# Four graph layers on one core: another load path for the neighbour counts, a pinned place for small loads, and another order for the last bank

## The chip, the cores and the metric

The kernel runs on one core of a Trainium2 chip. The metric is device time in microseconds for the whole program, the median of five runs. Beside it stands one profiled execution, whose trace gives every time quoted below: times in the trace count from the start of its span.

## The reference

Four layers work on x (3,327 nodes by 512 features) and one 0/1 adjacency matrix. Each layer's result is added to its input, and each row is then normed (mean taken off, divided by its deviation).

```
Layer 0 (attention, 8 heads of 64): Wh = x W; e[i,j] = leaky(f1[i] + f2[j]); where adj[i,j] > 0
        softmax over j, weights times Wh
Layer 1 (mean of neighbours): of each row keep the first 64 neighbours; nb = their mean of x;
        x <- norm(x + leaky(x Wl' + bl) + (leaky(nb Wn' + bn) where the row has a neighbour, else 0))
Layer 2 (as layer 0, other weights, then elu)
Layer 3 (as layer 2, 4 heads of 128)
```

Layer 1 needs for each row the number of its neighbours, as min(count, 64), its reciprocal, and whether it is above 0. These counts are what the change calls the neighbours' counts.

## The kernel before, in words

Rows are worked on in 26 tiles of 128 (NT = 26; the last tile holds 127 rows). A layer's attention runs over two halves of 13 tiles (HALF) of rows i and four slots s of 128 output features. One such (half, s) is a unit: it goes over all 26 tiles of neighbours j, makes a weight tile on VectorE (L403) and its sigmoid on ScalarE (L406), and multiplies on TensorE into the four banks `po` (L426, numerators) and the banks `pd` (L378, denominators). At a unit's end `po` is copied to `ob`, transposed by TensorE in groups of four tiles (`QUADS`: tiles 0 to 3, 4 to 7, 8 to 11 and 12) through `transposed` (L451), and either stored to `hd` in device memory (L464) or handed to `final` (L992). The denominators become `rec`, the reciprocals that the numerators are multiplied with.

TensorE's instructions keep the order in which they are written. All other engines and queues are ordered by a planner when the program is built, by priority in the order of writing and by its own idea of when inputs are ready; `tc.keep_in_program_order(ins)` pins an instruction behind the one written last on the same engine, without a wait for its end. An engine or a queue then works strictly in that order. SP issues DMAs from `nc.sync`, POOL those from `nc.gpsimd`.

**Start of layer 1** (`sage`, L676). The counts of all rows lie in device memory in row NT of `ctd`, as bf16. They are loaded by POOL into `cb` (L741) with rows on partitions, so each element goes to a place of its own, and turned into `cnt` on VectorE (L751 to L753); the first is pinned and written at tile 8. The loop from L745 takes tiles in twos. `finish` loads `h` and `xr` of the next two tiles (L126: the first group from POOL, later `h` from SP), multiplies with `rec` (L181), adds (L195), takes statistics (L152, L153) and norms (L154 to L161). `step1` transposes a tile on TensorE (L714) into the PSUM tile `pt`, of which there are two; `step2` of the tile before it makes two products (L722, L725) and stores `zd` and `xid`. In TensorE's order: step 1 of tile t, step 2 of tile t - 1.

**Late denominators.** For the last unit of layers 0 and 2 (`end` in `unit`) the denominators go out as `dd` (L505) and come back as `pes` by 16 small DMAs on SP (`place`, L508 to L515), written where the loop of the next stage (`sage`, or `third` at L907) has come to tile 4. At tile 8 `finish_sums` (L521 to L534, pinned) makes `rec` of the second half from them.

**Start of layer 3** (`third`, L878). The same pattern with `load_group` (L897), ten `h` buffers, `project1` (L251) and `project2` (L264), which stores `v` (L281) by SP; each normed tile is stored to x3 by SP (L133).

**The tail** (L992 to L1030). For layer 3's second half the finished output stays on chip in `g`; only slot s = 3 is left at the end. `take` divides a group out of PSUM into `h` (L999), takes exp (L1002), adds twice (L1004, L1005) and takes the row statistics (L1008, L1009). The groups 0 and 1 are transposed first, then `sums` and `reciprocals` make `rec` (L559 to L569), then the takes follow. After them come two blocks, tiles 0 to 7 and 8 to 12: one square root (L1019), two small steps for `rs` (L1020, L1021), and for each tile, from the last to the first, the scaling (L1026 on ScalarE for every fourth, else L1028 on VectorE) and the store (L133, L131; even tiles by SP, odd ones by POOL).

Of the kernel before, what the change touches and what calls it, by code (L numbers as in the profile page):

```python
# [18 lines left out]
P = 128  # L19
# [13 lines left out]
def kernel(  # L33
# [190 lines left out]
    class Layer:  # L224
# [137 lines left out]
        def unit(self, pools, half, s, background, aside, final=None, ending=None):  # L362
# [127 lines left out]
            if not by_pe:  # L490
# [17 lines left out]
                def place(pool=sp, tag="red", eng=nc.gpsimd):  # L508
                    pes = pool.tile([P, HALF, 2, 2, NS], F32, name="pes", tag=tag, bufs=1)
                    held.append(pes)  # L510
                    for kk in range(4):
                        q0, nq = (0, NA) if kk < 2 else (NA, HALF - NA)
                        src = dd[32 * kk:32 * kk + 32, :4 * nq].rearrange("i (q m) x -> m i q x", m=4)
                        for m in range(4):
                            eng.dma_start(out=pes[32 * m:32 * m + 32, q0:q0 + nq, kk % 2]  # L515
                                          .rearrange("p q o s -> p q (o s)"), in_=src[m])
# [54 lines left out]
            if not final:  # L571
# [3 lines left out]
            return [lambda: take.append(transposed(*QUADS[0])), lambda: take.append(transposed(*QUADS[1])),  # L575
                    sums, reciprocals] + [lambda q=q: take[q]() for q in range(2)] + \
                [lambda q=q: transposed(*q)() for q in QUADS[2:]]
# [98 lines left out]
    def sage(first, first_pool, xin, prev, nxt, wsrc, dst):  # L676
# [3 lines left out]
        with tc.tile_pool(name="sg_z", bufs=1, reuse_waits="tile") as zp, \  # L680
# [21 lines left out]
            with tc.tile_pool(name="sa_w", bufs=1, reuse_waits="tile") as wp, \  # L702
# [37 lines left out]
                cb = zp.tile([P, NT], BF, name="cb")  # L740
                nc.gpsimd.dma_start(out=cb, in_=ctd[NT:NT + 1, :].rearrange("o (t p) -> p (o t)", p=P))  # L741
# [3 lines left out]
                for t0 in range(0, NT, 2):  # L745
# [3 lines left out]
                    if t0 == 8:  # L749
                        tc.keep_in_program_order(  # L750
                            nc.vector.tensor_scalar(cnt[:, 0, :], cb, NEIGHBOURS, 1.0, op0=ALU.min, op1=ALU.max))  # L751
                        nc.vector.reciprocal(cnt[:, 1, :], cnt[:, 0, :])
                        nc.vector.tensor_scalar(cnt[:, 2, :], cb, 0.0, None, op0=ALU.is_gt)  # L753
# [124 lines left out]
    def third(first):  # L878
        with tc.tile_pool(name="col3", bufs=1) as cp, tc.tile_pool(name="at_r3", bufs=2, reuse_waits="tile") as rp:
# [51 lines left out]
            with tc.tile_pool(name="f3", bufs=2) as fp, tc.tile_pool(name="f4", bufs=1) as gp:  # L931
# [60 lines left out]
                def final(s, q0, n, pt):  # L992
# [4 lines left out]
                    def take():  # L997
                        h = fp.tile([P, 4, P], F32, name="h", bufs=2)
                        nc.vector.tensor_tensor(h[:, :n], pt[:, :n], rec[:, HALF + q0:HALF + q0 + n, s:s + 1]  # L999
                                                .to_broadcast([P, n, P]), op=ALU.mult)  # L1000
                        e = fp.tile([P, 4, P], F32, name="e")
                        nc.scalar.activation(e[:, :n], h[:, :n], AF.Exp)  # L1002
                        y = g[:, qs, s * P:(s + 1) * P]
                        nc.vector.scalar_tensor_tensor(y, e[:, :n], 1.0, y, op0=ALU.min, op1=ALU.add)  # L1004
                        nc.vector.scalar_tensor_tensor(y, h[:, :n], 0.0, y, op0=ALU.max, op1=ALU.add)  # L1005
                        if s == NS - 1:
                            for q in range(q0, q0 + n):
# [176 lines left out]
```

## Time and profile before

| What | us |
|---|---|
| median of 5 runs (lowest, highest) | 3392.05 (3390.57, 3394.94) |
| the profiled execution's own time | 3392.05 |
| its span | 3390.3 |
| PE busy | 3249.6 (96%) |
| DVE busy | 2684.2 (79%) |
| ACT busy | 2356.8 (70%) |
| last attention product of layer 0, start of layer 1 | about 957 |
| last product of layer 1's first loop's tile 0 | about 969.9 |
| last products of layer 3's attention | about 3360 |

PE is TensorE, DVE VectorE, ACT ScalarE, POOL GpSimd; SPq and POOLq are the queues of SP and POOL. A line of a timeline gives the start, the duration, the engine, the line of the kernel, the operation, the tile written and the tile read, the number of instructions, and in brackets the idle time before it with what ended it ("issue" where the view names nothing). A line of the waits gives who waited for what: total, times, longest.

### The profile page before, as it was taken

How to read it: one execution, taken by the hardware profiler on the slowest of the kernel's cores; microseconds unless marked ns; L12 is line 12 of the kernel's file. 1: busy time of each engine (PE TensorE's matmuls, PEld its weight loads, DVE VectorE, ACT ScalarE, POOL GpSimd, SP SyncE). 2: the span in 40 equal slices, each digit the busy share in tenths (PEclk: the TensorE clock that was granted, in tenths of full speed). 3: DMA queues.
4: the chain of work that ended last, by engine and by line, in shares of the span. 5: the costliest groups of instructions: out<-in, count | busy, mean ns of one | idle time of the engine just before them, and what ended most of it. 6: DMA issues, size and time to landing. Idle time of an engine off the chain costs nothing.

```text
span 3390.3 us, 47140 instructions
## 1 busy us (share of the span) xinstructions
PE 3249.6 (96%) x18423; PEld 1626.5 (48%) x18475; DVE 2684.2 (79%) x2615; ACT 2356.8 (70%) x2142; POOL 241.7 (7%) x390
## 2 busy tenths in 40 slices
PE   8799999999979999999989999999998999999997
PEld 7544344444434445545544444444446754445453
DVE  5799999999967544444449999999998766668886
ACT  2398998999953333333329999999997755558985
POOL 3100000000010011111110000000002000010110
PEclk9999999999989999999999999999999999999998
DMA  9644111110143343333320111111117411122311
GB/s 372 216 126 126 49 49 39 57 46 28 44 122 120 116 122 88 90 83 87 84 77 19 48 50 48 50 50 42 38 32 238 155 41 42 41 51 78 96 42 49
DMA packets 288055, 284.29 MB, mean 84 GB/s; under 512 B 107533, under 2 KB 223575, under 8 KB 287832
## 3 DMA queue, kind: packets, MB, share of 16 engines
q1 hardware_dynamic: 254024, 170.61, 16.7%
q0 software_dynamic: 28288, 102.97, 9.7%
q10 hardware_dynamic: 5520, 7.69, 0.7%
q8 instruction: 146, 2.39, 0.3%
q14 instruction: 77, 0.63, 0.1%
HBM read 212.01 MB, written 69.17 MB: 83 GB/s over the span
## 4 chain that ended last, share of the span: by engine, by line
PE 84%; DVE 4%; DMA 4%; issue 4%; ACT 3%; POOL 0%; SPq 0%; ACTq 0%; POOLq 0%; DVEq 0%
PE po L426 50%; PE acc L845 12%; PE pd L378 7%; PE pw L269 5%; DVE t L403 3%; PE pz L722 3%; PE pi L725 3%; DMA raw<-in_adjT_dram 2%; ACT y L406 1%; PE pk L805 1%; PE pt L454 1%; DMA asb<-in_a_dram 0%; PE pa L1066 0%; PE pt L259 0%; PE pt L714 0%
## 5 line engine op out<-in xcount | busy, mean ns | idle before, releaser
L403 DVE SCALAR_TENSOR_TENSOR t<-rb,qc,mask 128x1664 f32<-128x1664 f32 x1040 | 1959.1, 1949 | 169.4 <-PE po L426 148.3
L406 ACT ACTIVATE y<-t,bi,sc 128x1664 fp8e4<-128x1664 f32 x1040 | 1769.8, 1766 | 309.7 <-PE pd L378 290.7
L426 PE MATMUL po<-t,vj 128*64 128x448 f32 (+3 forms) x8320 | 1909.5, 520 | 24.2 <-DVE t L403 24.0
L426 PEld LDWEIGHTS po<-t,vj 128*64 128x64 f32 (+1 forms) x8320 | 838.4, 148 | 973.1 <-issue 700.5
L845 PE MATMUL acc<-zs,kt 128*128 128x512 bf16 x1312 | 394.9, 382 | 2.2 <-issue 0.2
L845 PEld LDWEIGHTS <-kt 128*128 128x128 fp8e4 x2002 | 196.8, 98 | 242.4 <-issue 9.3
L269 PE MATMUL pw<-wsb,xT 128*128 128x264 f32 (+1 forms) x1248 | 299.3, 395 | 14.0 <-DVE vt L275 12.5
L797 ACT CAST pk<-cy 128x512 f32<-128x512 bf16 x169 | 99.2, 588 | 278.9 <-DVE kt L809 272.6
L378 PE MATMUL pd<-y,sden 128*32 128x448 fp8e4 (+1 forms) x4160 | 259.3, 341 | 10.4 <-ACT y L406 10.4
L269 PEld LDWEIGHTS pw<-wsb,xT 128*128 128x128 f32 x1248 | 239.9, 196 | 57.8 <-issue 8.8
L845 PE MATMUL acc<-zl,kt 128*128 128x512 bf16 x638 | 241.8, 379 | 0.6
L378 PEld LDWEIGHTS <-sden 128*32 128x32 bf16 x4160 | 117.4, 96 | 162.6 <-issue 139.8
L809 DVE SCALAR_TENSOR_TENSOR kt<-pk,mask 128x512 fp8e4<-128x512 f32 x169 | 116.1, 687 | 96.5 <-PE pk L805 96.5
L275 DVE TENSOR_TENSOR vt<-pw,dc 128x256 f32<-128x256 f32 x156 | 59.2, 418 | 148.7 <-ACT dc L270 142.6
L357 POOL DMA_DIRECT2D rb<-r x40 | 21.3, 534 | 1686.2 <-DVE t L403 1664.7
L273 ACT COPY rc<-pw 128x8 f32<-128x8 f32 (+1 forms) x78 | 12.7, 163 | 155.9 <-PE pw L269 153.4
L817 DVE SCALAR_TENSOR_TENSOR y<-acc,cnt,bnb 128x512 f32<-128x512 f32 x26 | 19.5, 751 | 96.7 <-PE acc L845 89.3
L690 POOL DMA_DIRECT2D cy<-ctd x91 | 67.9, 746 | 385.6 <-ACT pk L797 311.8
L722 PE MATMUL pz<-wn,xT 128*128 128x512 f32 x208 | 95.0, 600 | 0.4 <-ACT xT L716 0.4
L725 PE MATMUL pi<-wl,xT 128*128 128x512 f32 x208 | 93.5, 592 | 0.0
L624 DVE TENSOR_SCALAR mask<-raw 128x832 fp8e4<-128x832 int32 (+2 forms) x90 | 53.9, 605 | 39.9 <-DMA raw<-in_adjT_dram 39.7
L154 ACT ACT_TABLE_LOAD x46 | 59.0, 1283 | 37.0 <-DVE mv L153 36.4
(185 smaller groups left out, 1702.7 us busy)
## 6 DMA issues: line engine op xcount, KB each, us to landing
vj<-v SPq DMA_DIRECT2D x312, 128.0 KB
rb<-r POOLq DMA_DIRECT2D x40, 832.0 KB, 4.8
raw<-in_adjT_dram SPq DMA_DIRECT2D x67, 416.0 KB
cy<-ctd POOLq DMA_DIRECT2D x78, 256.0 KB, 4.1
h<-hd SPq DMA_DIRECT2D x61, 256.0 KB
v<-vt SPq DMA_DIRECT2D x50, 256.0 KB
hd<-hb SPq DMA_DIRECT2D x48, 256.0 KB
xr<-x POOLq DMA_DIRECT2D x45, 256.0 KB, 3.1
```

Source lines behind the costliest of these rows:

```text
L269: nc.tensor.matmul(pw[e][:, :FW + H], xT[:, c, :], wsb[:, c, e, :], start=c == 0, stop=c == FC - 1)
L275: nc.vector.tensor_tensor(vt[:, hs, :], pw[e][:, :FW].rearrange("p (h d) -> p h d", d=D), self.dc[:, t, hs].rearrange("p (h e) -> p h e", e=1)
L378: nc.tensor.matmul(pd[c][32 * kk:32 * kk + 32, :w_], lhsT, rhs, start=(kk, c) not in seen, skip_group_check=final is not None, stop=last a ...
L403: nc.vector.scalar_tensor_tensor(t, rb[k], self.qc[:, j, h:h + 1], mask[:, j, i0:i0 + IW], op0=ALU.max, op1=ALU.mult)
L406: nc.scalar.activation(y, t, AF.Sigmoid, bias=self.bi[:, j, h:h + 1], scale=self.sc[:, j, h:h + 1], saturate=False)
L426: nc.tensor.matmul(po[c][k * D:(k + 1) * D, :z - a_], vj[:, j % 2, k * D:(k + 1) * D], ts[k][:, a_:z], start=j == 0, stop=j == NT - 1)
L690: nc.gpsimd.dma_start(out=cy[:, :n, :], in_=ctd[t:t + n, b * GW:(b + 1) * GW] .rearrange("(o t) i -> o t i", o=1).to_broadcast([P, n, GW]))
L722: nc.tensor.matmul(pz, xT[:, c, :], wn[:, c, :], start=c == 0, stop=c == FC - 1)
L725: nc.tensor.matmul(pi, xT[:, c, :], wl[:, c, :], start=c == 0, stop=c == FC - 1)
L797: nc.scalar.copy(pks[k % 2], carry[b, t // 4 * 4][:, t % 4:t % 4 + 2, :])
L809: nc.vector.scalar_tensor_tensor(kt, pk, NEIGHBOURS, mask[:, t:t + 2, i0:i0 + GW], op0=ALU.is_le, op1=ALU.mult, saturate=False)
L845: nc.tensor.matmul(acc, kts[t][:, s * P:(s + 1) * P], zs(t, c) if c < 2 else zl[:, t, :], start=t == 0 and c == 0, stop=t == NT - 1 and c ...
```

## The change

Three parts.

1. The counts are loaded by SP instead of POOL into `cr`, 26 rows of 128, each row one run of 256 bytes. At tile 8 ScalarE makes a float32 copy, TensorE transposes it into a `pt` tile in PSUM, and the three VectorE instructions read it there. The pin of the first of them is gone.
2. In `place`, the first of the 16 `pes` loads of an `end` unit is pinned behind what is written before it on its queue.
3. The tail. The jobs of the last unit are reordered: each group's divide is followed by the transposes of the group two ahead. The divides are pinned one after the other, then the four exps; then group by group the two adds, the statistics and the square root, with the scaling and the stores of the group before between them, all pinned. The tiles of a group are scaled and stored in rising order, and groups 2 and 3 have buffers of their own for `h` and `e`.

```diff
-                            eng.dma_start(out=pes[32 * m:32 * m + 32, q0:q0 + nq, kk % 2]
-                                          .rearrange("p q o s -> p q (o s)"), in_=src[m])
+                            ins = eng.dma_start(out=pes[32 * m:32 * m + 32, q0:q0 + nq, kk % 2]
+                                                .rearrange("p q o s -> p q (o s)"), in_=src[m])
+                            if end and kk + m == 0:
+                                tc.keep_in_program_order(ins)
...
-            return [lambda: take.append(transposed(*QUADS[0])), lambda: take.append(transposed(*QUADS[1])),
-                    sums, reciprocals] + [lambda q=q: take[q]() for q in range(2)] + \
-                [lambda q=q: transposed(*q)() for q in QUADS[2:]]
+            def step(k):
+                if k < len(QUADS):
+                    take.append(transposed(*QUADS[k]))
+            jobs = [lambda: step(0), lambda: step(1), sums, reciprocals]
+            for k in range(len(QUADS)):
+                jobs += [lambda k=k: take[k](), lambda k=k: step(k + 2)]
+            return jobs
...
-                cb = zp.tile([P, NT], BF, name="cb")
-                nc.gpsimd.dma_start(out=cb, in_=ctd[NT:NT + 1, :].rearrange("o (t p) -> p (o t)", p=P))
+                cr = fp.tile([NT, P], BF, name="cr", bufs=1)
+                nc.sync.dma_start(out=cr, in_=ctd[NT:NT + 1, :].rearrange("o (t p) -> (o t) p", p=P))
...
                     if t0 == 8:
-                        tc.keep_in_program_order(
-                            nc.vector.tensor_scalar(cnt[:, 0, :], cb, NEIGHBOURS, 1.0, op0=ALU.min, op1=ALU.max))
+                        cf = fp.tile([NT, P], F32, name="cf", bufs=1)
+                        nc.scalar.copy(cf, cr)
+                        pt = ps.tile([P, FC, P], F32, name="pt")
+                        cb = pt[:, 0, :NT]
+                        nc.tensor.transpose(cb, cf, ident[:NT, :NT])
+                        nc.vector.tensor_scalar(cnt[:, 0, :], cb, NEIGHBOURS, 1.0, op0=ALU.min, op1=ALU.max)
...
+                def scale(q0, n):
+                    qs = slice(q0, q0 + n)
+                    keep(nc.vector.reciprocal(rs[:, qs, 0], rs[:, qs, 0]))
+                    keep(nc.vector.scalar_tensor_tensor(rs[:, qs, 1], mv[:, qs, 0], -1.0, rs[:, qs, 0],
+                                                        op0=ALU.mult, op1=ALU.mult))
+                    for q in range(q0, q0 + n):
                         y = g[:, q, :]
                         if q % 4 == 3:
+                            keep(nc.scalar.activation(y, y, AF.Identity, bias=rs[:, q, 1:2], scale=rs[:, q, 0:1]))
                         else:
+                            keep(nc.vector.tensor_scalar(y, y, rs[:, q, 0:1], rs[:, q, 1:2], op0=ALU.mult, op1=ALU.add))
                         store(y, HALF + q, q)
+                for _, _, exp, _, _ in lasts:
+                    keep(exp())
+                for k, (q0, n, _, add1, add2) in enumerate(lasts):
+                    keep(add1())
+                    keep(add2())
+                    for q in range(q0, q0 + n):
+                        keep(nc.vector.bn_stats(out=st[:, q, 1, :], in_=g[:, q, FB:]))
+                        keep(nc.vector.bn_aggr(out=mv[:, q, :], in_=st[:, q, :, :]))
+                    keep(nc.scalar.activation(rs[:, q0:q0 + n, 0], mv[:, q0:q0 + n, 1], AF.Sqrt, bias=eps))
+                    if k > 0:
+                        scale(*lasts[k - 1][:2])
+                scale(*lasts[-1][:2])
```

## The prediction

> **What bounds the kernel now.** I read the page first: the busy shares, then the chain that ended last.
>
> ```profile
> PE 3249.6 (96%) x18423; PEld 1626.5 (48%) x18475; DVE 2684.2 (79%) x2615; ACT 2356.8 (70%) x2142; POOL 241.7 (7%) x390
> PE 84%; DVE 4%; DMA 4%; issue 4%; ACT 3%; POOL 0%; SPq 0%; ACTq 0%; POOLq 0%; DVEq 0%
> ```
>
> TensorE holds 84% of the chain, so a change pays only where PE stands idle. The diff touches three places where it may: the start of layer 1 (960 to 990 us), the start of layer 3's projection (2558 to 2640) and the tail (3365 to the end). For the first I asked for the waits between 955 and 1000 us (what waited, what ended it: total, times, longest; the SPq line is from the same view of SP's queue):
>
> ```profile
> PE pt L714 <- ACT h L161: 16.9, 1, 16.9
> POOL xr L126 <- issue: 10.6, 2, 10.4
> DVE cnt L753 <- DMA cb<-ctd: 8.1, 1, 8.1
> DVE h L181 <- DMA h<-hd: 4.2, 2, 3.4
> SPq L515 <- DMA dd<-red: 7.1, 1, 7.1
> ```
>
> PE loses 16.9 us in one piece, waiting for the norm of tiles 2 and 3. The timeline of POOL and DVE there shows who is late:
>
> ```profile
> 958.92 1.49 POOL L741 DMA_DIRECT2D cb<-ctd  x1
> 960.40 0.56 POOL L126 DMA_DIRECT2D h<-hd  x1
> 971.35 0.55 POOL L126 DMA_DIRECT2D xr<-in_x_dram  x1 [10.39 <-issue]
> ...
> 969.58 0.18 DVE L753 TENSOR_SCALAR cnt<-cb 128x26 f32<-128x26 bf16 x1 [8.13 <-DMA cb<-ctd]
> 970.56 0.69 DVE L181 TENSOR_TENSOR h<-h,rec 128x512 f32<-128x512 f32 x1 [0.80 <-DMA h<-hd]
> 974.52 0.69 DVE L195 TENSOR_TENSOR h<-h,xr 128x512 f32<-128x512 f32 x1 [3.27 <-DMA xr<-in_x_dram]
> 981.35 0.69 DVE L181 TENSOR_TENSOR h<-h,rec 128x512 f32<-128x512 f32 x1 [3.41 <-DMA h<-hd]
> 981.96 0.69 DVE L152 BATCH_NORM_STATS2 st<-h 128x6 f32<-128x512 f32 x1
> ```
>
> DVE stands 8.1 us for cb (10.6 us from issue to landing, though it is 6.7 KB). h of tile 2, queued behind cb, lands at 970.5. xr of tile 2 is stuck too: the trace's semaphore records show POOL waiting until 970.74 for the landing of an `hd` store issued at 961.86, whose buffer xr reuses. That store took 8.9 us, and on most DMA engines its increments came from 969 on. Then, with 16 `pes` loads on SP around the loads of tiles 4 and 5 (SP issues those at 975.77), DVE reaches L181 of tile 4 before L152 of tile 3 and waits for it until 981.35. Only then come mv, rs and L161 (985.92), and PE goes on at 986.79. From 987 to 1060 PE is busy without a gap, so time won before 987 is won at the end.
>
> **What the Trainium skill says.** "DMA: Bandwidth & Descriptors", Rules for kernel authors: a source or target whose last dimension isn't contiguous becomes one descriptor per element. cb is that (3,328 elements of 2 bytes), and the trace agrees: 10.6 us, against 2.0 us for one 7 KB `pes` load. Same page, Issuing engines are not separate DMA queues: transfers from all issuers share 16 engines. The trace agrees: SP's `hd` and `dd` transfers land late beside POOL's cb. "TensorE: Matmul & The Clock Gate", Part 1: an idle PE drops to half clock and must warm up. The trace agrees: granted clock 0.50 from 974 to 988, and eight pz matmuls took 4.82 us after the gap where 3.60 is usual. "ScalarE: Activation LUTs", Table sets: exp and sqrt need different sets; here a load is 1.28 us.
>
> **Part 1, counts.** Removed: the cb load and with it the 8.1 us DVE wait. Added: one load of 26 rows of 256 B on SP (0.3 to 0.6 us of issue), one ACT copy of 26x128 (at most the 0.27 us of the 128x128 hb copy), one PE transpose (0.27 us, as one L714 transpose), and L751 and L753 reading PSUM instead of SBUF (0.1 us more at most). The load is needed 60 us later and ACT and DVE idle there, so only PE's 0.2 to 0.3 us counts. Its `pt` buffer is one of two; step 1 of tile 9 takes the same one a tile (7.3 us) later, so the three DVE reads have that long.
>
> What does the gap become? Nothing but cb stands between blb and the loads of tile 2. In the records the first two `hd` stores land on most engines by 965.5 and 966.7 now; the rest follow them without cb by about 967.5. So xr(2) goes out at 967.7 instead of 971.35, and h(3) and xr(3) by 968.8. With the landing times of now (3.1, 3.4 and 3.9 us) xr(3) is there at 972.7 (976.35 now). Then L195 and L152 of tile 3, 0.69 each, and L153: mv at 974.2. Now 2.6 us pass from mv to L161, because DVE has L734, L195, L735 and L181 of others in between; I keep 1.5 of it. L161 takes 0.8: PE at 976.5, a gap of 6.6 us instead of 16.9. **Gain 10.3 us.** The clock still drops in 6.6 us (the third layer's gap of 6.19 did that), so nothing for warming up. Ends: all inputs early, with DVE's own work of about 7 us from 961.5 as the floor, gives PE at 970 to 972 and a warm clock: 15 + 1.7 = 16.5. If the store still holds xr, or DVE waits for h(4), PE starts at 983: 3.8.
>
> **Part 2, the pin on pes (L515).** The first of 16 `pes` loads now follows what was written last on SP: the xid store of tile 2 in layer 1, the v store of tile 2 in the third. In layer 1 this takes the loads from before h(4) to after 1005.5 (less the gain). They cost SP 10.9 us (5.15 + 5.73), and h(8) and h(9) queue behind: h(9) leaves 3.3 us later than its 1013.91. Tile 8's norm ended at 1022.8 and PE took it at 1032.3: 9.5 us of cover, so no loss. `rec` isn't needed until 1036. In the third they move from 2572.5 to 2590.6, and end by 2601.5. Then `rec` (L528, pinned on DVE at 2605.52) has its data at about 2603.5, 2 us in hand; h of tiles 14 to 17 leave up to 9 us late, for use at 2610.5 and later. DVE is full there (10.0 of 10 us from 2610 to 2620), so a late load costs one for one. I take +0.5 us; bounds -1 (SP free earlier, stores of x3 sooner) and +11.
>
> **Part 3, the tail.** Now, from the timeline:
>
> ```profile
> 3365.11 1.29 DVE L999 TENSOR_TENSOR h<-pt,rec 128x512 f32<-128x512 f32 x2
> 3371.01 0.64 DVE L999 TENSOR_TENSOR h<-pt,rec 128x512 f32<-128x512 f32 x1
> 3375.70 2.83 DVE L1028 TENSOR_SCALAR g<-g,rs 128x512 f32<-128x512 f32 x6
> 3378.86 1.91 DVE L1028 TENSOR_SCALAR g<-g,rs 128x512 f32<-128x512 f32 x4
> 3380.85 3.69 SPq L133 DMA_DIRECT2D out_dram<-g  x2
> ```
>
> DVE works until 3380.77, but 3.3 MB leave only from 3376.3 on; DMA is full at 323 to 356 GB/s until about 3387, and the span ends 3.1 us later. So the transfer bounds the tail. After: divides of quads 0 and 1 until 3366.4; PE's transposes of quad 2 ready at 3367.0 (five took 1.30 from 3365.95), divides done at 3367.9. Per quad of four: two adds 1.21, four stats and aggregates 1.06, the two rs steps 0.35, three scales 1.40. Quad 0: stats 3370.2. Quad 1: stats 3372.5, scales of 0 end 3374.2, first store near 3373.3. Quad 2: 3376.5, scales of 1 3378.2. Quad 3 (one tile): 3378.9, scales of 2 3380.7, its own 3381.5. ACT has its four exps by 3368.6 and one table load by 3369.9, before the first sqrt at 3370.2, so it adds nothing. The last store leaves in two pieces by about 3382.4 and lands 2.5 to 3.9 us later, at about 3385.2 instead of 3387.2 to 3387.5; with the same 3.1 us the span ends near 3388.0. **Gain 2.4 us**; bounds 0.5 (the tile of 112 + 15 rows, now last, is slow) and 3.5.
>
> **Sum.** 10.3 - 0.2 - 0.5 + 2.4 = 12.0 us off the span: 3390.3 to 3378.3. The profiled execution itself took 3392.05 us, 1.75 more than its span, and that equals the median of the five runs, so the forecast is 3380.0 us.
>
> **Rivals.** (B) The gap closes: 3392.05 - 16.5 - 2.4 + 0.7 = 3373.9. For it: without cb nothing but transfers holds tile 2. Against: 1.25 MB of wl and blb run until 963.8 and SP's stores moved only afterwards. (C) The stall is hidden in the other wait: xr still waits for the store and DVE for h(4), so taking cb away does little of what it says: 3392.05 - 3.8 - 2.4 + 0.7 = 3386.5. For it: the releaser of POOL was the store, not cb. Against: four of sixteen engines finished the second store 1.7 to 3.5 us after the others, at the time of cb. (D) The pin costs the third stage. One slip of 10.9 us, by the late h loads: 3380.0 + 10.9 = 3390.9, no change. Both `rec` and the h loads wait in turn: 21.8 less the 2 us in hand, 3399.8, slower. It decides from 18.8 us of PE idle more than the 14.6 that PE now waits for L161 between 2550 and 2660. Against: h loads run 8 us and more ahead of their use.
>
> **How the numbers follow.** Within 0.2% (6.8 us: 3385.3 to 3398.8) counts as no change; runs of this kernel spread by 4.4 us. Likeliest case 0.57 (its own range 3376.5 to 3383.5), B 0.15, C 0.14 (0.06 of it faster), D small 0.07, D large 0.07. Faster 0.57 + 0.15 + 0.06 = 0.78, same 0.08 + 0.07 = 0.15, slower 0.07. 3372 to 3387 holds all but D and the edges of C.
>
> **What would show it.** Right: the PE wait for L161 near 970 falls from 16.9 to about 6 us, no DVE wait for a count load, xr(2) issued near 968, SP's `pes` after the third xid store; output stores from 3373 (less the gain) and the last scale later than now relative to the first divide. Wrong: xr(2) still at 971, DVE waiting for h(4) ahead of L152, a DVE wait at L528 in the third stage or PE waits for L161 there well above 14.6, or output DMA still ending 22 us after the last `rec`.

## The result, and the profile after

The changed kernel takes 3388.19 us in the median (3381.94 to 3394.78), the kernel before 3393.02 us in the same comparison. The ratio is 0.9986, 95% interval 0.9981 to 0.9992: 4.8 us faster, between 2.7 and 6.4. That is less than the 0.2% that was called no change, and 7 us less than forecast. The profiled execution took 3389.41 us with a span of 3387.7.

The page of the changed kernel, shares and the chain that ended last:

```profile
PE 3248.2 (96%) x18424; PEld 1625.9 (48%) x18476; DVE 2686.6 (79%) x2619; ACT 2357.4 (70%) x2145; POOL 240.9 (7%) x389
PE 84%; DVE 5%; DMA 5%; ACT 3%; issue 2%; SPq 0%; POOL 0%; ACTq 0%; POOLq 0%; DVEq 0%
```

Nothing of the whole has moved; what there is to see lies in the stages. The waits between 945 and 1000 us of the changed kernel (total, times, longest; its lines in the first loop of layer 1 are 8 higher, so L722 was L714):

```profile
PE pt L722 <- ACT h L161: 13.9, 1, 13.9
POOL xr L126 <- issue: 10.3, 1, 10.3
DVE h L181 <- DMA h<-hd: 7.9, 2, 6.0
```

The wait for cb is gone from VectorE, the wait of POOL ahead of xr has hardly changed (10.4 before), VectorE waits for h instead, and TensorE's piece is 13.9 us instead of 16.9. The count load in runs is waited for by ScalarE alone (7.0 us, until 969.08). The copy of tile 0's `pz` stands behind it and so starts at 969.30, 3.9 us after `pz` was ready; VectorE uses that copy only at 977.27, so nothing waits for it. The timeline of the same stretch, all engines:

```profile
967.96 3.85 SPq L515 DMA_DIRECT2D pes<-dd  x6
968.77 0.54 POOL L126 DMA_DIRECT2D xr<-in_x_dram  x1 [10.31 <-issue]
...
971.91 1.01 SPq L126 DMA_DIRECT2D h<-hd  x2
971.91 0.69 DVE L195 TENSOR_TENSOR h<-h,xr 128x512 f32<-128x512 f32 x1 [4.77 <-DMA xr<-in_x_dram]
...
972.97 5.52 SPq L515 DMA_DIRECT2D pes<-dd  x9
...
975.95 0.69 DVE L181 TENSOR_TENSOR h<-h,rec 128x512 f32<-128x512 f32 x1 [1.93 <-DMA h<-hd]
976.55 0.69 DVE L195 TENSOR_TENSOR h<-h,xr 128x512 f32<-128x512 f32 x1
...
979.07 0.17 DVE L153 BATCH_NORM_AGGREGATE mv<-st 128x2 f32<-128x6 f32 x1
```

Times of this trace and of the one before can't be laid over each other as they stand: tile 0's product, behind which TensorE begins to wait, ends at 968.84 here and at 969.87 there.

Two things contradict the forecast. Of the 16 `pes` loads, 15 are still around the h loads on SP: only one is held back, to 1001.56, the others are put where the planner likes. Six stand ahead of h of tiles 4 and 5 (971.91), and VectorE's L181 of tile 4 (975.95, the line with 1.93 us of idle) stands ahead of L195 of tile 3. And POOL issues xr of tile 2 only at 968.77: the semaphore records show it waiting until 968.15 for the last increment of an `hd` store issued at 960.89. (In the records the landing of such a store is 16 increments of a semaphore.)

The tail of the changed kernel, first and last of each kind:

```profile
3362.95 1.29 DVE L1016 TENSOR_TENSOR h<-pt,rec 128x512 f32<-128x512 f32 x2
...
3367.16 0.29 DVE L1063 BATCH_NORM_STATS2 st<-g 128x6 f32<-128x128 f32 x1
3367.49 0.21 DVE L1064 BATCH_NORM_AGGREGATE mv<-st 128x2 f32<-128x12 f32 x1
...
3372.80 8.91 SPq L133 DMA_DIRECT2D out_dram<-g  x6
...
3381.66 0.55 DVE L1054 TENSOR_SCALAR g<-g,rs 128x512 f32<-128x512 f32 x1
3382.23 1.16 SPq L131 DMA_DIRECT2D out_dram<-g  x2
```

The stores start earlier, 9.9 us after the first divide instead of 11.2. But VectorE's chain from the first divide to the end of the last scale is 19.3 us long; before it was 15.7. One stats and aggregate pair takes 0.40 to 0.46 us from start to start, where before it was 0.26 to 0.27. From the last product of attention to the end of the span it is 30.8 us; before it was 31.0.

By stages, the profiled executions differ by 3.05 us in TensorE's piece and by 0.2 us in the tail, both to the good. Against that stand 1.8 us in layer 3's attention (669.6 against 667.8 us), where no instruction changed its place. Kernels below that have the same code there show 667.7 to 671.7, so that lies within chance.

### The profile page after: what moved, and what is told of

It is laid out like the page before. It is cut to its first block, busy times and chain, and to the rows that moved or that the text cites. A ratio compares the mean times of both kernels' runs of the same rounds, so it can differ in the third digit from the quotient of the medians.

```text
span 3387.7 us, 47136 instructions
## 1 busy us (share of the span) xinstructions
PE 3248.2 (96%) x18424; PEld 1625.9 (48%) x18476; DVE 2686.6 (79%) x2619; ACT 2357.4 (70%) x2145; POOL 240.9 (7%) x389
## 4 chain that ended last, share of the span: by engine, by line
PE 84%; DVE 5%; DMA 5%; ACT 3%; issue 2%; SPq 0%; POOL 0%; ACTq 0%; POOLq 0%; DVEq 0%
PE po L426 50%; PE acc L857 12%; PE pd L378 7%; PE pw L269 5%; DVE t L403 3%; PE pz L730 3%; DMA raw<-in_adjT_dram 3%; PE pi L733 3%; ACT y L406 2%; PE pt L454 1%; PE pk L817 1%; DMA h<-hd 0%; PE pt L259 0%; PE pa L1105 0%; DMA out_dram<-h 0%
## 5 line engine op out<-in xcount | busy, mean ns | idle before, releaser
L426 PE MATMUL po<-t,vj 128*64 128x448 f32 (+3 forms) x8320 | 1909.9, 520 | 25.0 <-DVE t L403 24.7
L426 PEld LDWEIGHTS po<-t,vj 128*64 128x64 f32 (+1 forms) x8320 | 838.3, 148 | 974.5 <-issue 702.8
L269 PE MATMUL pw<-wsb,xT 128*128 128x264 f32 (+1 forms) x1248 | 298.1, 393 | 14.2 <-DVE vt L275 12.7
L378 PE MATMUL pd<-y,sden 128*32 128x448 fp8e4 (+1 forms) x4160 | 259.4, 341 | 10.4 <-ACT y L406 10.4
L269 PEld LDWEIGHTS pw<-wsb,xT 128*128 128x128 f32 x1248 | 239.1, 195 | 57.5 <-issue 8.7
```

What stands on the lines that cost most here:

```text
L269: nc.tensor.matmul(pw[e][:, :FW + H], xT[:, c, :], wsb[:, c, e, :], start=c == 0, stop=c == FC - 1)
L378: nc.tensor.matmul(pd[c][32 * kk:32 * kk + 32, :w_], lhsT, rhs, start=(kk, c) not in seen, skip_group_check=final is not None, stop=last a ...
L426: nc.tensor.matmul(po[c][k * D:(k + 1) * D, :z - a_], vj[:, j % 2, k * D:(k + 1) * D], ts[k][:, a_:z], start=j == 0, stop=j == NT - 1)
```

## The experiments

Times are medians; ratios are to the kernel before, measured in the same comparison. "Wait" is TensorE's longest wait at the start of layer 1, "stage 3" the time in layer 3's projection from the first product of the second group of tiles to the last one of L269, "tail" the time from attention's last product into `po` (L426) to the end of the span. Labels of runs have their numbers, 1 to 17.

| Kernel | wait | stage 3 | tail | median | ratio (95%) |
|---|---|---|---|---|---|
| before | 16.9 | 110.6 | 31.0 | 3393.02 | 1 |
| changed | 13.9 | 110.5 | 30.8 | 3388.19 | 0.9986 (0.9981, 0.9992) |
| 1 counts alone | 14.1 | 110.0 | 30.7 | 3389.60 | 0.9994 (0.9986, 1.0002) |
| 2 tail alone | 17.1 | 109.8 | 31.4 | 3392.57 | 0.9997 (0.9988, 1.0005) |
| 3 pin alone | 16.9 | 109.6 | 30.9 | 3392.23 | 1.0000 (0.9992, 1.0009) |
| 4 no wait for cb | 17.4 | 110.3 | 30.8 | 3391.40 | 1.0000 (0.9992, 1.0008) |
| 5 all pins | 11.4 | 110.7 | 30.4 | 3385.36 | 0.9981 (0.9973, 0.9989) |
| 6 staggered tail | 14.5 | 110.4 | 29.4 | 3387.29 | 0.9982 (0.9976, 0.9989) |
| 7 wl late | 12.4 | 110.3 | 30.5 | 3386.94 | 0.9984 (0.9978, 0.9991) |
| 8 = 5 + 6 + 7 | 11.6 | 110.5 | 28.6 | 3384.23 | 0.9979 (0.9970, 0.9988) |
| 9 = 5 + blb late | 11.0 | 110.3 | 30.4 | 3388.37 | 0.9986 (0.9980, 0.9993) |
| 10 = 5 + hb on y | 10.9 | 112.3 | 30.3 | 3393.70 | 1.0001 (0.9993, 1.0009) |
| 11 = 6 + 9 + 10 | 11.5 | 112.8 | 28.9 | 3392.40 | 0.9998 (0.9990, 1.0006) |
| 12 = 5 + 6 | 11.4 | 109.6 | 28.9 | 3382.68 | 0.9975 (0.9965, 0.9986) |
| 13 = 5, quarter of wl | 11.6 | 110.4 | 30.6 | 3385.13 | one run |
| 14 = 9 + 13 | 11.6 | 109.5 | 30.8 | 3384.73 | one run |
| 15 = 12, h of 4 tiles late | 11.6 | 110.4 | 28.8 | 3386.43 | 0.9979 (0.9970, 0.9988) |
| 16 = 12, h of 2 tiles late | 11.4 | 110.1 | 28.6 | 3386.31 | 0.9980 (0.9974, 0.9986) |
| 17 = 12 + VectorE pinned | 9.4 | 110.2 | 28.9 | 3382.52 | 0.9965 (0.9951, 0.9978) |

The whole time of a kernel spreads by 8 us and more from run to run, so a single stage is judged by its own length in the trace. The wait repeats within 0.6 us where the kernel's start of layer 1 is the same (16.9 to 17.1 in before, 2 and 3; 13.9 to 14.5 in changed, 1 and 6; 11.4 in 5 and 12).

### Each part alone

Run 1 is the kernel before with the hunks of part 1, run 2 with those of the tail, run 3 with the pin.

> The kernel before with the counts part alone (loads of pes and the tail as before). Theory W: what is left of TensorE's idle piece at the start of layer 1 comes from stores that leave late behind the 1.25 MB of wl and blb and from pes loads of SP ahead of h(4), and the pin adds nothing to that; so this kernel has the whole gain of that piece: TensorE waits 13.9 us for L161 (16.9 before, 13.9 after the whole change), about 3 us off the time. Rival P: the pin took part in it (the first of the sixteen pes loads is later), so without it the wait stays at 15 us or more and the time falls by 2 us or less. By the prediction's sum it would be 6.6 us and 10 off.

> The kernel before with the tail part alone. Theory S: the pinned order lets VectorE's dependent pairs stand back to back, which makes its chain from the first divide to the last scale about 19.3 us long (15.7 before), and that eats the earlier start of the stores: from the end of the last attention to the end of the span 30.8 us against 31.0, time unchanged within 1 us. Rival, the prediction's part 3: 2.4 us less (28.6). If layer 3's attention is 1.8 us longer here too (669.6 against 667.8), the new order costs something ahead of the tail as well; if not, that difference between the two profiled executions was chance.

> The kernel before with the pin on the first pes load alone. Theory N: one of sixteen loads moves, the rest float as before: time the same within 1 us, TensorE's wait for L161 at the start of layer 1 16.9 us, the third stage 110.5 us. Rival: by itself the pin costs or gains in the third stage, whose length then leaves 110.5 by more than 1 us.

The counts have the whole gain at the start of layer 1 (14.1 us), as theory W had it; the pin adds nothing and costs nothing; the tail alone gains nothing (31.4 us, its chain 19.2 us as in the changed kernel). All three intervals take in no change. By their ratios the parts give -2.0, -1.0 and 0 us (by their medians -3.6, -0.6 and -1.0), the whole -4.8; stages account for 3.3. The rest isn't resolved, and needn't be anything: the intervals overlap.

### The transfer of cb, or the wait for it

```diff
-                        nc.vector.tensor_scalar(cnt[:, 2, :], cb, 0.0, None, op0=ALU.is_gt)
+                        tc.keep_in_program_order(
+                            nc.vector.tensor_scalar(cnt[:, 2, :], cb, 0.0, None, op0=ALU.is_gt))
```

> The kernel before, in which only the third VectorE operation on the counts (L753) is pinned to tile 8, so that VectorE doesn't wait for cb at the start of layer 1, while cb is still loaded element by element at the same place. Theory T: it is the transfer of cb that costs (it stands ahead of h(2) in POOL's queue and takes DMA engines from the stores), so TensorE's wait for L161 stays at 16 to 17 us and the time doesn't change. Rival V: it is VectorE's 8.1 us for cb, so the wait falls by about 3 us, to 13.9, as in the counts part.

The waits of run 4, 945 to 1000 us:

```profile
PE pt L714 <- ACT h L161: 17.4, 1, 17.4
DVE h L181 <- DMA h<-hd: 12.0, 2, 8.2
```

VectorE no longer waits for cb; it waits for h of tile 2 instead, and then for xr of tile 2, which it has 4.7 us after the end of tile 0's product, as before. Theory T: the 8.1 us line was a wait behind which another stood. What cost was the transfer of cb. The view by stretches shows it (start and end, length, busy time of PE, PEld, DVE, ACT and POOL, TensorE's clock, busy share of the DMA engines, GB/s), first in the kernel before, then at the same place in the changed one:

```profile
966.00:968.00 2.00, 2.00 (x7) 0.80 (x6) 0.00 (x0) 0.59 (x1) 0.00 (x0) 1.00 0.99 81
965.00:967.00 2.00, 2.00 (x6) 0.81 (x5) 0.55 (x1) 0.00 (x0) 0.00 (x0) 1.00 1.04 316
```

While cb passes, the engines are as busy as without it and move a quarter of the bytes. SP's store packets take 5.3 us from the first to the last in the changed kernel, 7.4 before. They don't start later before: 4.4 us after the first store's issue, 4.9 in the changed kernel. That cb also stood ahead of h in POOL's queue cost nothing by itself, as xr came later still.

### All sixteen pes loads pinned

```diff
-                            if end and kk + m == 0:
+                            if end:
```

> The changed kernel with all sixteen pes loads pinned in place of the first alone. Theory W: the six pes loads that SP still issues ahead of h(4) hold VectorE at L181 of tile 4, which stands before L195 of tile 3; with all sixteen behind, h(4) leaves SP about 8 us earlier, xr(3) becomes the last input, and TensorE's wait for L161 falls from 13.9 to about 11.7 us, 2 us off the time. Rival O: h(4) isn't what decides (xr of tile 3 lands at the same moment), and the wait stays at 13.5 or more. In the third stage the loads go late as a block as the prediction feared: if rec or the h loads come late, the stage exceeds 112 us (110.5 now).

The timeline of run 5, all engines:

```profile
961.79 4.18 SPq L126 DMA_DIRECT2D h<-hd  x4
...
966.75 0.54 POOL L126 DMA_DIRECT2D xr<-in_x_dram  x1 [9.71 <-DMA h<-hd]
970.15 0.69 DVE L195 TENSOR_TENSOR h<-h,xr 128x512 f32<-128x512 f32 x1 [6.00 <-DMA xr<-in_x_dram]
...
975.16 0.17 DVE L153 BATCH_NORM_AGGREGATE mv<-st 128x2 f32<-128x6 f32 x1
```

SP issues four h loads at 961.79 instead of two at 971.91, VectorE no longer waits for tile 4, and the wait falls by 2.4 us: theory W. The third stage stays at 110.7 us, so a block of loads there, which rival D feared, costs nothing. This is what the prediction took the change itself to do.

### Stats and aggregates apart

```diff
                     for q in range(q0, q0 + n):
                         keep(nc.vector.bn_stats(out=st[:, q, 1, :], in_=g[:, q, FB:]))
+                    for q in range(q0, q0 + n):
                         keep(nc.vector.bn_aggr(out=mv[:, q, :], in_=st[:, q, :, :]))
```

> The changed kernel with one thing in the tail altered: for each group of quads all stats are issued first and then all aggregates, so that no aggregate follows its own stats. Theory S: a dependent pair costs VectorE 0.40 us and a staggered one 0.27, over 13 tiles 1.7 us, so the chain from the first divide to the last scale falls from 19.3 to about 17.5 us and the end comes 1 to 1.7 us earlier. Rival, the DMA bound of the prediction's part 3: the output transfer sets the end whatever VectorE does, the chain gets shorter and the end stays where it was relative to the end of attention (30.8 us) within 0.4.

The timeline of run 6, VectorE:

```profile
3364.23 1.29 DVE L1016 TENSOR_TENSOR h<-pt,rec 128x512 f32<-128x512 f32 x2
...
3368.44 0.87 DVE L1063 BATCH_NORM_STATS2 st<-g 128x6 f32<-128x128 f32 x4
3369.23 0.41 DVE L1065 BATCH_NORM_AGGREGATE mv<-st 128x2 f32<-128x12 f32 x4
3369.55 0.64 DVE L1025 SCALAR_TENSOR_TENSOR g<-e,g 128x512 f32<-128x512 f32 x1
...
3381.30 0.55 DVE L1054 TENSOR_SCALAR g<-g,rs 128x512 f32<-128x512 f32 x1
```

Four tiles take 1.11 us instead of 1.66, the chain 17.6 us instead of 19.3, and the end comes 1.4 us earlier. Theory S; the transfer isn't the bound here. All later kernels with this edit have tails of 28.6 to 28.9 us.

### What keeps the stores and xr late

Run 7 moves the loads of wl and blb behind those of tiles 2 and 3 on POOL, run 8 joins it with runs 5 and 6.

```diff
-                wl = load_w(wp, wlT, "wl", nc.gpsimd)
+                wl = wp.tile([P, FC, F], F32, name="wl")
...
-                nc.gpsimd.dma_start(out=blb, in_=bl.to_broadcast([P, F]))
...
+                            if t0 == 0:
+                                tc.keep_in_program_order(
+                                    nc.gpsimd.dma_start(out=wl, in_=wlT.rearrange("(c p) m -> p c m", p=P)))
+                                nc.gpsimd.dma_start(out=blb, in_=bl.to_broadcast([P, F]))
```

> The changed kernel with the loads of wl and blb (1.25 MB) issued on POOL behind the h and xr loads of tiles 2 and 3 instead of ahead of them. Theory W: SP's hd stores then leave at once, POOL gets past its wait for the store near 963 instead of 968, the inputs of tiles 2 and 3 are there by 970, and the wait moves to wl itself, which tile 0's own product needs (some 6 us there); the two idle pieces together come to 8 to 10 us instead of 14.8, about 5 us off the time, at most 8. Rival: the store is slow in itself (write receipt), POOL still waits until 967 or later, and wl comes on top: slower by 4 us or more.

> The last three edits together. If they are independent the time is the changed kernel's less their three gains: by theory W and S 8 us less (2 + 1.5 + 5), near 3380. If all pins and the late wl buy the same wait (both bring the inputs of tile 3 forward), it is no better than the late wl and the staggered tail alone, 6 us less.

Theory W of run 7 falls. Only the pinned wl moved; blb and the cy load went ahead of h. The wait is now for wl at tile 0's own product, 12.4 us long. Counted from the first store's issue, xr of tile 2 goes out after 9.2 us, in the changed kernel after 10.5: the stores gained 1.3 us, not the 5 of theory W. Nor was the kernel slower, as the rival had it. Run 8 shows the gains of runs 5 and 6 and no more.

Three kernels on top of all pins each took one of the suspects away. Run 9 loads blb last; run 10 gives the last stored tile another buffer, so that xr doesn't lie on it:

```diff
-                    hb = vp.tile([P, n, P], F32, name="hb", tag="vj")
+                    hb = yp.tile([P, n, P], F32, name="hb", tag="y")
```

> All sixteen pes loads pinned as in the fifth run, and the load of blb (one row of 2 KB read by 128 partitions) issued on POOL behind the h and xr loads of tiles 2 and 3 instead of behind wl. In the run with the late wl, blb stayed ahead and its 4096-byte packets took up to 753 ns each, against 159 for those of wl. Theory B: it is this load that keeps the stores of SP back, so without it they leave some 2 us earlier, xr of tile 2 is issued near 8 us after wl instead of 11.5, and TensorE's wait for L161 falls from 11.4 to about 9.5 us. Rival R: the stores' own time and receipts set it (in the late-wl run POOL still waited as long), the wait stays at 11 or more.

> All sixteen pes loads pinned, and the buffer of the last hd store (hb of the odd tile) taken from the ring of y instead of vj, so that xr of tile 2 no longer lies on it; that store's landing is then waited for by h of tile 5 instead. Theory H: the buffer alone holds xr back; POOL issues xr(2), h(3), xr(3) at once behind h(2), VectorE is next held by L181 of tile 4 (h(4) lands near 968 in this clock), and TensorE's wait for L161 falls from 11.4 to about 8 us, the time by about 3 us against the fifth run. Rival C: the loads now run against the stores, h(4) lands later by as much, and the wait stays at 11 or more.

> All of these together with the staggered stats and aggregates of the tail: all pes loads pinned, hb on y, blb late. If the pieces add up: TensorE's wait for L161 7 us or less, tail 29.4 us (30.8 in the changed kernel), some 7 + 1.4 us less than the changed kernel, near 3380; if blb and the buffer are two names for one wait, near 3382.

Runs 9 and 10 each give about 0.5 us at the wait (rivals R and C, or nearly), no more than the 0.6 us by which it repeats. The timeline of run 10 shows why it gave so little:

```profile
958.64 0.54 POOL L126 DMA_DIRECT2D xr<-in_x_dram  x1
...
966.46 5.34 SPq L126 DMA_DIRECT2D h<-hd  x4
966.92 0.69 DVE L195 TENSOR_TENSOR h<-h,xr 128x512 f32<-128x512 f32 x1
...
971.89 1.29 DVE L181 TENSOR_TENSOR h<-h,rec 128x512 f32<-128x512 f32 x2 [4.28 <-DMA h<-hd]
```

xr of tile 2 is issued some 10 us earlier, and L195 has it at 966.92. But now xr's bytes pass ahead of SP's stores, SP's h loads go out 2.6 us before the end of tile 0's product instead of 5.6 (run 5), and VectorE stands for h of tile 4 until 971.89: rival C. The same edit also moved buffers at the start of layer 3. There 17.9 us pass from the first product to the second group's, 12.0 in run 5, which "stage 3" doesn't count; the whole projection is 8 us longer (134.3 against 126.6), and that makes runs 10 and 11 as slow as the kernel before. So run 11 misses its 3380 to 3382 at both places: its wait is 11.5 us, and it has the loss in layer 3.

Runs 13 and 14 load only a quarter of wl, run 14 also blb behind. They leave out three parts of four of the line product's weights and stand for the transfers alone.

```diff
-                wl = load_w(wp, wlT, "wl", nc.gpsimd)
+                wl = wp.tile([P, FC, F], F32, name="wl")
+                nc.gpsimd.dma_start(out=wl[:, 0, :], in_=wlT[:P, :])
...
-                        nc.tensor.matmul(pi, xT[:, c, :], wl[:, c, :], start=c == 0, stop=c == FC - 1)
+                        nc.tensor.matmul(pi, xT[:, c, :], wl[:, 0, :], start=c == 0, stop=c == FC - 1)
```

> All sixteen pes loads pinned, and of wl only the first 256 KB of 1 MB loaded, used for all four chunks of the inner dimension of the line product (so that product is left out in three parts of four); TensorE's work and all else stay. It takes 0.75 MB out of the transfers ahead of the stores. Theory B: bytes set what is left of the piece; at the 350 to 400 GB/s of that window 0.75 MB are 2 us, so the stores and xr(2) come about 2 us earlier and TensorE's wait for L161 falls from 11.4 to about 9.5 us. Rival L: the chain of latencies (store, its landing, xr, its landing) sets it whatever else is moved, and the wait stays at 11 or more.

> The last run's kernel (a quarter of wl loaded, the line product left out in three parts of four) with the load of blb behind the h and xr loads too. Ahead of the stores POOL's queue then holds 0.75 MB and no slow broadcast: one load of wl, one of cy and h(2), 256 KB each. Elsewhere in the changed kernel a lone hd store of 256 KB has its first packet 0.9 us after its issue and its last 3.1 us after it. Theory Q: SP's stores wait for POOL's queue to drain, so they start 1 to 2 us sooner after their issue than in the last runs (3.4 us and more after it), and xr(2) is issued 9 us after wl instead of 11.5. Rival L: the stores start and end when they did, xr(2) is issued 10.5 us or more after wl. The order of VectorE's operations shifts a little with the loads, so the reading is that of the stores and of xr(2), not of TensorE's wait.

The wait stays at 11.6 us in both. In the packet records SP's first 512-byte store packet comes 4.9 us after the first store's issue in the changed kernel, 4.8 in run 5, 3.4 in run 13 and 3.1 in run 14, where a lone store has 0.9. (Over all kernels it is 3.1 to 3.5 us in the four with three quarters of wl or more out of the way, 4.0 to 5.2 in the others.) So the stores do start later with more ahead of them in POOL's queue. xr of tile 2 went out 10.2 us after wl in run 14, between theory Q (9) and rival L (10.5). But then 4.4 us passed to L195 (3.4 in run 5), behind SP's four h loads, and 4.2 from the second L153 to TensorE (3.6), and nothing was left of the gain.

Runs 15 and 16 put those h loads behind xr, on POOL (run 16, with `t0 > 2`, only those of tiles 4 and 5):

```diff
-                            ahead = finish(fp, xin, prev, t0 + 2, 2, 6, nc.sync if t0 else nc.gpsimd)
+                            ahead = finish(fp, xin, prev, t0 + 2, 2, 6, nc.sync if t0 > 4 else nc.gpsimd)
```

> All sixteen pes loads pinned, staggered tail (as in the twelfth run), and h of tiles 4 to 7 loaded by POOL behind xr of tile 3 instead of by SP ahead of it. In the runs with all pins SP's four h loads (1 MB) pass the DMA engines between the stores and xr of tiles 2 and 3, whose landing then takes 3.4 to 4.4 us (3.05 in the changed kernel). Theory T, a train of transfers: with these four behind, xr(2) and xr(3) land right after the stores, VectorE has L195 of tile 3 near 971 instead of 973, and TensorE's wait for L161 falls from 11.4 to 8 or 9 us; the tiles behind may then wait a little for h(4), so the time falls by 1 to 3 us against the twelfth run. Rival L: latencies alone set it, the wait stays at 11. Rival G: the wait falls, but as much is given back at tiles 4 to 7, and the time stays.

> The same with only h of tiles 4 and 5 on POOL; those of tiles 6 and 7 stay on SP, so 0.5 MB stand between the stores and xr. Theory T: the wait for L161 lies between the two, near 9.5 to 10 us. Rivals as in the run with all four.

From xr's issue to L195 it was 3.1 and 3.0 us, and the wait stayed at 11.6 and 11.4. Theory T falls here: transfers delay one another, but the last link before TensorE isn't a transfer.

### The order on VectorE

From L195 of tile 2 to the second L153, VectorE works without a break in run 5: 5.0 us, 1.8 of it on tiles 0 and 4. Then 3.6 us pass to TensorE. Run 12 joins runs 5 and 6; run 17 is run 12 with VectorE's instructions of tiles 2 and 3 pinned first, then those of tile 0's product, then tiles 4 and 5.

```diff
+    def stay(ins):
+        if hold[0]:
+            tc.keep_in_program_order(ins)
...
-            nc.vector.bn_stats(out=st[:, s, :], in_=y)
+            stay(nc.vector.bn_stats(out=st[:, s, :], in_=y))
...
+                            hold[0] = t0 < 4
                             ahead = finish(fp, xin, prev, t0 + 2, 2, 6, nc.sync if t0 else nc.gpsimd)
+                            hold[0] = False
```

> The changed kernel with all sixteen pes loads pinned and with the staggered stats and aggregates: the two edits that each shortened their own stage. They lie 2400 us apart, so they should add: TensorE's wait for L161 11.4 us, the tail 29.4 us, and about 2.4 + 1.4 us less than the changed kernel, near 3384.5, ratio to the kernel before about 0.9975. If one of the two was worth nothing, 0.9982 as in either run alone.

> All sixteen pes loads pinned and the staggered tail (as in the twelfth run), and VectorE's operations at the start of layer 1 pinned: L181, L195, L152, L153, L155, L158 of tiles 2 and 3 first, then those of tile 0's product (r, z, xi), then L181 and L195 of tiles 4 and 5. Theory V: what is left above the forecast of 6.6 us is, with all pins, 1.2 to 1.8 us of store, and 3 us of VectorE's order: 5.0 us pass from L195 of tile 2 to the second L153 with four operations of other tiles in between, where the forecast took 3.4, and 3.6 us from there to TensorE, where it took 2.3. So with this order the first falls to 4 us or less, the second to 3 or less, and TensorE's wait from 11.4 to 9.2 to 9.8 us, the time by about 2 us against the twelfth run. Rival W: VectorE then only waits for xr of tile 3, and the wait for L161 stays above 10.5 us. Rival G: the wait falls, and tile 0's product, now later, gives it back at tile 3 or 4.

The timeline of run 17 (its lines are 6 higher than those of before here: L201 is L195, L159 is L153, L160 is L154):

```profile
972.17 1.28 ACT L160 ACT_TABLE_LOAD   x1
974.46 0.69 DVE L201 TENSOR_TENSOR h<-h,xr 128x512 f32<-128x512 f32 x1 [6.35 <-DMA xr<-in_x_dram]
...
979.47 0.17 DVE L159 BATCH_NORM_AGGREGATE mv<-st 128x2 f32<-128x6 f32 x1
979.68 0.30 ACT L160 ACTIVATE rs<-mv,eps 128x2 f32<-128x2 f32 x1 [6.23 <-DVE mv L159]
```

Run 12 is what its two parts promised. In run 17 the wait falls to 9.4 us, as theory V had it in sum, though not in its shares. The way from L195 to the second L153 is still 5.0 us: the work on tiles 0 and 4 is gone from it, but 0.65 us of waiting for xr of tile 3 came in its place and 1.2 us for L187 (L181 before) of tiles 6 and 7, which the pins leave free and which wait on the semaphores of those tiles' loads. From there to TensorE it is 1.85 us instead of 3.64. In the changed kernel the table load for the square root stood on ScalarE behind a copy that waited for tile 0's `r` and came at 978.63; here it is done long before mv. And L155 and L158 follow at once instead of behind two operations of other tiles. Rival G isn't excluded: from tile 0's product to the end of layer 1's first loop it is 194.7 us, in run 12 195.5, so 0.8 of the 2.0 us are seen there; but the loop behind the wait differs by 1.1 us between executions of the same code (183.3 in the changed kernel, 184.4 in run 6). Run 17 has the lowest median and ratio of the study, 0.9965 (0.9951 to 0.9978), and beats both kernels; against run 12 its intervals overlap.

## Why the prediction was wrong

The wait for cb that the change removed cost nothing by itself, and of the forecast gain of 12.0 us, 4.8 came by the medians and 3.3 by the stages. Two of the prediction's sums are a little off, 15 + 1.7 (16.7) in the bound of part 1 and 3385.2 + 3.1 (3388.3, a gain of 2.0) in part 3; neither decides anything below.

**Part 1, the gap.** Its mechanism held in part (cb among the stores; its place ahead of h cost nothing), its size didn't. The forecast's chain had four links. With times from the end of tile 0's last product (when TensorE begins to wait), L153 taken at its start (in the forecast at its end, some 0.1 us later):

| | xr(2) issued | to L195 of tile 2 | to second L153 | to TensorE | wait |
|---|---|---|---|---|---|
| before | +1.5 | 3.2 | 8.6 | 3.6 | 16.9 |
| forecast | -2.2 | 3.1 | 3.4 | 2.3 | 6.6 |
| changed | -0.1 | 3.1 | 7.2 | 3.6 | 13.9 |
| run 5 | -0.6 | 3.4 | 5.0 | 3.6 | 11.4 |
| run 17 | -0.9 | 3.4 | 5.0 | 1.9 | 9.4 |

The first step that failed is "the rest follow them without cb by about 967.5". The stores were not late by cb alone: of the 3.7 us that xr was to gain, taking cb away brought 1.6, and xr went out 2.1 us later than forecast. Of these, 0.7 us are the fifteenth of the store's 16 increments (967.14, where the forecast, brought to this trace, has 966.5 for all), 1.0 the last one (968.15), and 0.4 the way from there to xr's issue, 0.6 us in both kernels where the forecast took 0.2. The stores' late start behind POOL's loads stayed as it was. The second is in part 2, that the change "takes the loads from before h(4) to after 1005.5". It took one of sixteen, and 2.2 us of the third link are that; run 5 shows it by doing what the forecast assumed. The third is "Then L195 and L152 of tile 3, 0.69 each, and L153": it laid one tile's operations end to end on a VectorE that had others queued between them, 1.6 us in run 5 (1.8 us of work on tiles 0 and 4). The fourth, "I keep 1.5 of it", was an assumption with no line under it: the 2.6 us from mv's end to L161 are 2.6 in the changed kernel too, and did not shrink until the order was pinned (0.8 in run 17). The forecast saw this interleaving in the trace of before ("L734, L195, L735 and L181 of others in between") and credited the change with undoing it, though no hunk touches it. Together 2.1 + 3.8 + 1.3 = 7.2 us, all but 0.1 of 13.9 - 6.6.

Why the stage resisted single remedies: runs 7, 9, 10, 13, 14, 15 and 16 each took one late thing away and gained 0.5 us or less at the wait of their base, or moved it. The reading that fits them all is that stores, h, xr and VectorE's order were late within 1 to 2 us of one another. How much of the 9.4 us of run 17 the stores' late start still sets was not taken apart further.

**Part 2, the pin.** No cost in the third stage, as forecast within its half microsecond (110.5 against 110.6). That is not its mechanism come true: the loads did not move as a block. Run 5 moved them, and the stage stayed at 110.7. But the reading of the hunk was wrong, as above: a condition on `kk + m == 0` pins one load.

**Part 3, the tail.** Forecast 2.4 us, found 0.2 in the profile and nothing in run 2. The step that failed is "four stats and aggregates 1.06" and "two adds 1.21": rates of the old order, in which neighbouring instructions belonged to different tiles, put into an order in which each depends on the one before. Measured, a group takes 1.66 and 1.44 us. Three groups and the single tile make that 2.8 us more: the chain is 19.3 us where 16.4 was forecast. The stores did start earlier; the last one didn't. Its own range ended at 0.5, a little above what came. That "the transfer bounds the tail" was wrong as well for the new order: run 6 shortens VectorE by 1.6 us and the end follows by 1.4.

**The rivals.** C came nearest (3386.5): a stall hidden in the other wait, with xr behind the store and VectorE at h(4). It had 0.14. Its argument, that POOL's releaser was the store and not cb, was the better reading. Of its two signs in the list, VectorE's wait for h(4) came true (1.93 us); xr's issue moved, but by less than half of what was forecast. B asked for a stage without a second cause; D never arose.

## What to carry to other kernels

A wait in the list is worth its length only if nothing else of the same stage lands in the same microseconds: before crediting its removal, list every input of the instruction that TensorE waits for, with its landing and its place in its queue, and cost the next latest; run 4 removed the longest such wait of VectorE for nothing. Compare two traces by times counted from an event of the stage itself. Read a pin for what it binds, one instruction, and ask where its siblings float to. Durations taken from a stream of independent instructions don't hold for a dependent chain: where an order is written out by hand, alternate tiles (all stats, then all aggregates).

## What the runs showed of the hardware

- A load element by element (cb, 6.7 KB) held the DMA engines: from 966 to 968 us they were 99% busy in the kernel before and moved 81 GB/s, at the same place in the changed one 104% and 316 (the view's share can pass 100%). Single packets of SP's `hd` and `dd` transfers took up to 1.0 to 2.0 us in the four kernels with cb, at most 0.09 in the others.
- Two queues that share the 16 DMA engines did not get equal turns. In the changed kernel SP's first store packets come at 963.2, 4.9 us after their issue, as POOL's run of 4096-byte packets nears its end; a store of the same form alone starts after 0.9 us and ends after 3.2 (median of 56). In run 10 both went side by side from 963.6 to 967.4, SP with some 50 packets of 512 bytes in half a microsecond, where it had 225 to 300 afterwards. It goes the other way too: with SP's h loads ahead, 4.4 us passed from xr's issue to L195 (run 14) instead of 3.1.
- A load that repeats one row of 2 KB over 128 partitions (blb, 256 KB) was slow. With nothing ahead of it in POOL's queue it landed 5.3 us after its issue (run 7), a quarter of wl, 256 KB too, 2.9 us (runs 13 and 14). The first 64 of POOL's packets behind the issue took 312 ns in the median and up to 1504 in run 7 (not up to 753, as the expectation of run 9 has it), 159 in the median in runs 13 and 14.
- A landing is that of the slowest engine. Of the 16 increments of the store that POOL waited for, 15 had come by 967.14 in the changed kernel and the last at 968.15; in run 14 the last came 1.3 us after the others. The packet records have a transfer beside these stores that the argument doesn't count, in every kernel: 16 KB of instructions, 0.9 us long, at 963.89 in the changed kernel. There the last increment comes 1.0 to 1.1 us behind the fifteenth at all four stores, and within 0.1 us at the six `pes` loads issued from 967.96 to 971.21. That the late engine is the one with the instructions fits this, but isn't shown: the records don't name the engine.
- On VectorE a stats and aggregate pair on 128x128 cost 0.40 us with the aggregate behind its own stats and 0.28 with four of each in a row; two dependent adds on 128x512 took 1.44 us, two independent ones 1.21. The Trainium skill, "VectorE: DVE Perf Modes", The DRAIN you can't avoid, has chained copies as long with a semaphore after each as with one at the end. No run here repeats that measurement; between these small neighbours it was dependence that cost, 0.12 us a pair, and for this order the runs decide.
